# Moving the column transform and the tile sum to later places in TensorE's order

## The chip, the cores and the metric

The kernel runs on one core of a Trainium2 chip. Its time is the device time of one execution in microseconds (us). The kernel before takes 4047.03 us (median of three runs, 4043.34 to 4052.0).

## The reference

Eight images of 8 channels and 256 x 256 pixels go through a Fourier layer network and then through a dilation. Cut to what matters here:

```python
h = _gconv1x1(h, fc0_w, fc0_b)
for i in range(4):
    h1 = _spectral_conv(h, sp_w1[i], sp_w2[i])   # rfft2, mix of 2 x 12 x 12 modes, irfft2
    h2 = _gconv1x1(h, w_w[i], w_b[i])            # 4 groups of 10 channels
    h = h1 + h2
    if i < 3:
        h = _gswish(h, betas[i])
h = _gswish(_gconv1x1(h, fc1_w, fc1_b), betas[3])   # 10 -> 128 per group
return _gconv1x1(h, fc2_w, fc2_b)                   # 128 -> 2 per group
...
x = x + _L0_conv_ref(_gn(x), ...)
x = x + _L1_conv_ref(_gn(x))     # maximum over 3 x 3 windows
```

The kernel does the transforms as matrix products with cosine and sine tables. Within the loop over layers each pixel chunk of layer l gets its new values, and at once the row-wise (width) part of the forward transform that layer l + 1 needs: this is what the change moves.

## The kernel before

An image has 11 chunks of pixels (`NCH = 11`). For layers 0 to 2 each chunk goes through these parts:

- `burst(c)`, TensorE: 16 matmuls of the 1x1 convolution (L480, in layer 0 L477) and 8 of the inverse transform (L483) into two PSUM tiles; ScalarE then applies SiLU into `h` (L489).
- `turn(c)`, VectorE: transposes the chunk in 32 x 32 blocks into one of three slots of `turned` (L431).
- `transform(k)`, TensorE: for pair k (chunks 2k and 2k + 1) 32 matmuls of 32 x 32 into two PSUM tiles (L448), copied to `e` in a slot of `turned`, one by VectorE (L201) and one by ScalarE (L199).
- `gather(k)`, TensorE: four matmuls with stacked unit matrices that sum the four row tiles of `e` (L462), copied to `zt` by VectorE (L465 or L468). This is the tile sum.

```python
def ps_z(name):
    return ps.tile([128, 2, 512], F32, tag="z", bufs=4, name=name)
...
def transform(k):
    cs = chunks_of(k)
    ...
    pair = [ps_z(f"p_d_{b}_{l}_{k}_{i}") for i in range(2)]
    for v in range(8):
        for q in range(NQ):
            mm(pair[q // 2][part(v % 4), q % 2, : 240 * n], fw8[part(q), v, :],
               t[part(q), :, :, v, : NBLK * WID], start=v < 4, stop=v >= 4)
    e = turned[:, (2 * k + 1) % 3, : 960 * n].rearrange("p (q x) -> p q x", q=NQ)
    for i in range(2):
        copy_2(i, e[:, 2 * i : 2 * i + 2], pair[i][:, :, : 240 * n])

def gather(k):
    ...
    e = turned[:, (2 * k + 1) % 3, : 960 * n].rearrange("p (q r f i) -> p q r f i", q=NQ, r=2 * n, f=NQ)
    p = ps_a(f"p_u_{b}_{l}_{k}")
    for g in range(NQ):
        m = e[:, :, :, g] if group_in_f else e[:, g].rearrange("p q r i -> p r q i")
        mm(p[part(g), : 240 * n], stack, m, start=True, stop=True)
    ...

def burst(c):
    pair = [ps_z(f"p_z_{b}_{l}_{c}_{i}") for i in range(2)]
    for f in range(NQ):
        for q in range(NQ):
            o = pair[q // 2][part(f), q % 2, :]
            ...
                mm(o, wt[part(q), l, g, :], h[part(q), c, f, :], start=True, stop=False)
    for s in range(2):
        for q in range(NQ):
            mm(pair[q // 2][:, q % 2, HW * s : HW * (s + 1)],
               zt[part(q), 2 * c + s].rearrange("p f o -> p (f o)"), binv[part(q), :],
               start=False, stop=s == 1)
    for i in range(2):
        ...
            nc.scalar.activation(dst, pair[i], AF.Silu)
```

`ps_a` is the first bank of a `ps_z` tile. [...] While image b + 1 goes through the layers, the head of image b (fc1 and fc2) and its dilation run in between: each `yield` of a layer hands over to the main loop, which puts in steps of the head.

```python
for n in layers(b, stored, d, start(b + 1, ahead)):
    if isinstance(n, str):                 # "even"/"odd": bring the count of steps to that parity
        if count[0] % 2 != (n == "odd") and step():
            share -= 1.0
    elif isinstance(n, tuple):             # (1,): one step exactly, and a bit of the dilation
        exact += sum(n)
        for _ in range(sum(n)):
            if scale and step():
                tail()
    else:                                  # a number: a share of a step
        loose += n
        share += n * scale if scale else 0
        while share >= 1.0:
            share -= 1.0
            step()
scale = scale or (STEPS - exact) / loose   # STEPS = 128 steps per image
```

In image 0 there is no head yet, and no step is put in. An odd step is `first(n)`: 4 matmuls of fc1 (L628) into two PSUM tiles, with SiLU by ScalarE (L630). An even step is `second(n - 4)`, 8 matmuls of fc2 (L650) whose result VectorE adds to `y` (L655), and then a `first(n)`. In the trace an fp32 matmul has two rows, so fc1 is x8, fc2 x16, the transform x64, the tile sum x8.

Of the kernel before, what the change touches and what calls it, by code (L numbers as in the profile page):

```python
# [33 lines left out]
NCH = 11  # L34
# [10 lines left out]
def fno_dilate_kernel(ctx: ExitStack, tc: tile.TileContext, a: dict, out: bass.AP):  # L45
# [10 lines left out]
    def ps_z(name):  # L56
        return ps.tile([128, 2, 512], F32, tag="z", bufs=4, name=name)

    def ps_a(name):
        return ps_z(name)[:, 0, :]  # L60

    def part(i):
        return slice(32 * i, 32 * i + 32)
# [133 lines left out]
    def copy_2(i, dst, src):  # L197
        if i % 2:
            nc.scalar.activation(dst, src, AF.Identity)  # L199
        else:  # L200
            nc.vector.tensor_copy(dst, src)  # L201
# [146 lines left out]
    def load_sw(l, k):  # L348
        t = sb.tile([128, G, 2 * WID, WID], F32, tag="sw")
        nc.sync.dma_start(t.rearrange("p g m i -> p (g m i)"), a["spw"][l, k])  # L350
        return t
# [72 lines left out]
    def layer(b, l, out_, stored, side):  # L424
        group_in_f = l % 2 == 1

        def turn(c):

            dst = turned[:, c % 3].rearrange("p (s f x) -> p f s x", s=2, f=NQ)
            for i in range(2):  # L430
                nc.vector.transpose(  # L431
                    dst[:, 2 * i : 2 * i + 2], h[:, c, 2 * i : 2 * i + 2].rearrange("p f (s x) -> p f s x", s=2))

        def chunks_of(k):

            return sorted(range(2 * k, min(2 * k + 2, NCH)), key=lambda c: c % 3)

        def transform(k):


            cs = chunks_of(k)
            n, lo = len(cs), cs[0] % 3
            step = cs[-1] % 3 - lo if n == 2 else 1
            t = turned[:, lo : lo + step * (n - 1) + 1 : step].rearrange("p n (r v i) -> p n r v i", r=2 * NQ, v=8)
# [12 lines that stand above are left out]
            n = len(cs)  # L457
# [5 lines that stand above are left out]
            src = p[:, : 240 * n].rearrange("p (r g i) -> p r g i", r=2 * n, g=G)  # L463
            if cs == sorted(cs):
                nc.vector.tensor_copy(zt[:, 4 * k : 4 * k + 2 * n, :, : NBLK * WID], src)  # L465
            else:
                for i, c in enumerate(cs):
                    nc.vector.tensor_copy(zt[:, 2 * c : 2 * c + 2, :, : NBLK * WID], src[:, 2 * i : 2 * i + 2])  # L468
# [6 lines that stand above are left out]
                    if l == 0:  # L475
                        k = slice(32 * q, 32 * q + 6)
                        mm(o, wcn[k, :], h[k, c, f, :], start=True, stop=False)  # L477
                    else:
                        g = f if group_in_f else q
# [7 lines that stand above are left out]
                dst = h[:, c, 2 * i : 2 * i + 2, :]  # L487
                if l < 3:
                    nc.scalar.activation(dst, pair[i], AF.Silu)  # L489
                else:  # L490
                    nc.scalar.activation(dst, pair[i], AF.Identity, bias=bias3)  # L491
            if l == 3:
                nc.sync.dma_start(stored[c], h[:, c].rearrange("p f w -> p (f w)"))
# [19 lines left out]
                yield (LAST,)  # L513
            return
        yield "even"
        for c in range(NCH):
            k = c // 2
            if c % 2 == 0:
                burst(c)
                yield (1,)  # L520
                turn(c)
                if k > 0:
                    transform(k - 1)
            else:
                burst(c)
                if k > 0:
                    gather(k - 1)
                yield (1,)
                turn(c)
        out_["sw"] = [load_sw(l + 1, 0), load_sw(l + 1, 1)]  # L530
        yield 1
        gather(k - 1)
        transform(k)
        yield 2
# [10 lines left out]
    def layers(b, stored, d, then):  # L545

        for l in range(4):  # L550
            if l > 0:
                yield from spectrum_h(b, l, d)
                yield from mix(b, l, d)
            yield from rows_of(b, l)
            yield from layer(b, l, d, stored, then if l == 3 else iter(()))
        yield from then
# [367 lines left out]
```

## Time and profile before

| engine | busy us | share of the span |
|---|---|---|
| TensorE, matmul (PE) | 3734.7 | 92% |
| TensorE, weight load (PEld) | 1463.3 | 36% |
| ScalarE (ACT) | 2853.1 | 71% |
| VectorE (DVE) | 2538.8 | 63% |
| GpSimd (POOL) | 117.0 | 3% |

The profiled execution spans 4041.6 us at a mean TensorE clock of 0.977 of full speed. The costliest groups of instructions:

| line | engine | what | count | busy us | mean ns |
|---|---|---|---|---|---|
| L630 | ScalarE | SiLU behind fc1 | 2048 | 1960.1 | 1026 |
| L628 | TensorE | fc1 | 8192 | 1204.4 | 631 |
| L650 | TensorE | fc2 | 8192 | 997.5 | 601 |
| L431 | VectorE | turn | 528 | 623.2 | 1219 |
| L483 | TensorE | burst, inverse transform | 5632 | 411.7 | 405 |
| L480 | TensorE | burst, 1x1 convolution | 8448 | 371.1 | 601 |
| L448 | TensorE | column transform | 9216 | 309.9 | 540 |
| L462 | TensorE | tile sum | 1152 | 137.3 | 546 |
| L201 | VectorE | copy of the transform | 144 | 152.1 | 1057 |
| L199 | ScalarE | copy of the transform | 144 | 130.1 | 903 |

Busy time of overlapping matmuls is the time in which at least one of a group runs, so the busy times of lines are not additive. A mean of a line mixes its shapes: the last transform of a layer has one chunk only, and half the columns. How long TensorE is kept by a group of matmuls is read from the start of the group to the start of the next.

### The profile page before, as it was taken

How to read it: one execution, taken by the hardware profiler on the slowest of the kernel's cores; microseconds unless marked ns; L12 is line 12 of the kernel's file. 1: busy time of each engine (PE TensorE's matmuls, PEld its weight loads, DVE VectorE, ACT ScalarE, POOL GpSimd, SP SyncE). 2: the span in 40 equal slices, each digit the busy share in tenths (PEclk: the TensorE clock that was granted, in tenths of full speed). 3: DMA queues.
4: the chain of work that ended last, by engine and by line, in shares of the span. 5: the costliest groups of instructions: out<-in, count | busy, mean ns of one | idle time of the engine just before them, and what ended most of it. 6: DMA issues, size and time to landing. Idle time of an engine off the chain costs nothing.

```text
span 4041.6 us, 118640 instructions
## 1 busy us (share of the span) xinstructions
PE 3734.7 (92%) x53530; PEld 1463.3 (36%) x53530; DVE 2538.8 (63%) x3535; ACT 2853.1 (71%) x2991; POOL 117.0 (3%) x202
## 2 busy tenths in 40 slices
PE   5666999999999999999999999999999999999997
PEld 2333333433333333333433333333333333333221
DVE  6765656556766666766666666666676666673533
ACT  3334777777777777777777777777777777778886
POOL 1000000000000000000000000000000000000000
PEclk8888999999999999999999999999999999999998
DMA  3005111432125321252122611144121532215311
GB/s 85 14 14 188 53 33 41 139 123 58 58 67 166 93 59 58 82 189 56 55 64 89 197 44 53 53 134 151 55 59 51 164 109 63 61 48 194 96 53 46
DMA packets 113985, 345.05 MB, mean 85 GB/s; under 512 B 15768, under 2 KB 18392, under 8 KB 98056
## 3 DMA queue, kind: packets, MB, share of 16 engines
q1 hardware_dynamic: 95288, 276.33, 22.0%
q0 software_dynamic: 18192, 61.13, 4.7%
q8 instruction: 422, 6.91, 0.7%
q14 instruction: 83, 0.68, 0.1%
HBM read 213.40 MB, written 123.74 MB: 83 GB/s over the span
## 4 chain that ended last, share of the span: by engine, by line
PE 78%; DVE 11%; ACT 7%; issue 3%; DMA 1%; POOL 0%; DVEq 0%; POOLq 0%; SPq 0%; ACTq 0%
PE p_fc L650 22%; PE p_fc L628 20%; PE p_z L483 8%; PE p_z L480 7%; PE p_d L448 6%; ACT act L630 4%; PE p_u L462 3%; PE p_z L477 3%; DVE turned L431 2%; PE p_b L333 2%; PE p_g L405 2%; PE p_g L410 2%; ACT h L491 2%; DVE turned L324 2%; DVE turned L201 1%
## 5 line engine op out<-in xcount | busy, mean ns | idle before, releaser
L630 ACT ACTIVATE act<-p_fc 128x1024 f32<-128x1024 f32 x2048 | 1960.1, 1026 | 669.6 <-PE p_fc L628 665.3
L628 PE MATMUL p_fc<-hs,c_w 32*128 32x512 f32 x8192 | 1204.4, 631 | 14.8 <-DVE turned L195 8.5
L650 PE MATMUL p_fc<-act,c_w 128*32 128x512 f32 x8192 | 997.5, 601 | 47.1 <-ACT act L630 35.5
L628 PEld LDWEIGHTS p_fc<-hs,c_w 32*128 32x128 f32 x8192 | 402.3, 183 | 697.3 <-ACT act L630 278.5
L489 ACT ACTIVATE h<-p_z 128x1024 f32<-128x1024 f32 x528 | 511.7, 1021 | 190.5 <-PE p_z L483 189.8
L431 DVE STREAM_TRANSPOSE turned<-h 128x1024 f32<-128x1024 f32 x528 | 623.2, 1219 | 23.4 <-ACT h L489 23.1
L655 DVE TENSOR_TENSOR y<-p_fc,y 128x512 f32<-128x512 f32 x392 | 270.6, 690 | 497.1 <-PE p_fc L650 496.1
L650 PEld LDWEIGHTS p_fc<-act,c_w 128*32 128x32 f32 x8192 | 227.5, 109 | 645.6 <-issue 345.5
L483 PE MATMUL p_z<-c_binv,zt 32*128 32x256 f32 x5632 | 411.7, 405 | 0.6 <-ACT zt L193 0.6
L480 PE MATMUL p_z<-h,c_wt 32*32 32x512 f32 x8448 | 371.1, 601 | 6.7 <-DVE y L655 3.4
L483 PEld LDWEIGHTS p_z<-c_binv,zt 32*128 32x128 f32 x5632 | 261.6, 186 | 305.4 <-issue 295.8
L448 PE MATMUL p_d<-turned,c_fw 32*32 32x480 f32 (+1 forms) x9216 | 309.9, 540 | 11.1 <-DVE turned L431 11.1
L195 DVE COPY zt<-p_g 128x264 f32<-128x264 f32 x300 | 162.6, 629 | 167.1 <-PE p_g L410 91.6
L491 ACT ACTIVATE h<-p_z,c_bias 128x1024 f32<-128x1024 f32 x176 | 186.5, 1111 | 38.8 <-PE p_z L483 38.4
L199 ACT ACTIVATE turned<-p_d 128x960 f32<-128x960 f32 x144 | 130.1, 903 | 94.5 <-PE p_d L448 94.5
L363 DVE TENSOR_REDUCE S<-turned 128x80 f32<-128x800 f32 x192 | 188.8, 983 | 4.7
L448 PEld LDWEIGHTS p_d<-turned,c_fw 32*32 32x32 f32 x9216 | 121.5, 103 | 187.1 <-issue 150.6
L360 DVE TENSOR_TENSOR turned<-t,B 128x800 f32<-128x800 f32 x192 | 188.6, 982 | 0.9 <-DMA t<-in_spw 0.8
L462 PE MATMUL p_u<-turned,c_stack 128*32 128x480 f32 (+1 forms) x1152 | 137.3, 546 | 42.9 <-DVE turned L201 42.9
L324 DVE STREAM_TRANSPOSE turned<-zt 128x960 f32<-128x960 f32 x96 | 175.6, 1857 | 0.6
L201 DVE COPY turned<-p_d 128x960 f32<-128x960 f32 x144 | 152.1, 1057 | 28.9 <-PE p_d L448 28.7
L480 PEld LDWEIGHTS p_z<-h,c_wt 32*32 32x32 f32 x8448 | 93.7, 103 | 211.2 <-ACT act L630 69.1
(169 smaller groups left out, 1964.8 us busy)
## 6 DMA issues: line engine op xcount, KB each, us to landing
stored<-h SPq DMA_DIRECT2D x88, 1024.0 KB
hs<-stored SPq DMA_DIRECT2D x352, 256.0 KB
t<-in_spw SPq DMA_DIRECT2D x96, 400.0 KB
yin<-y_rows POOLq DMA_DIRECT2D x56, 512.0 KB, 5.0
h<-in_xp SPq DMA_DIRECT2D x352, 48.0 KB
turned<-in_x SPq DMA_DIRECT2D x16, 1024.0 KB
y<-in_x SPq DMA_DIRECT2D x56, 256.0 KB
y_rows<-y POOLq DMA_DIRECT2D x56, 256.0 KB, 2.3
```

The source lines that it names most:

```text
L324: nc.vector.transpose(rows[:, 960 * g : 960 * (g + 1)].rearrange("p (i r) -> p i r", r=32), windows(g))
L431: nc.vector.transpose(dst[:, 2 * i : 2 * i + 2], h[:, c, 2 * i : 2 * i + 2].rearrange("p f (s x) -> p f s x", s=2))
L448: mm(pair[q // 2][part(v % 4), q % 2, : 240 * n], fw8[part(q), v, :], t[part(q), :, :, v, : NBLK * WID], start=v < 4, stop=v >= 4)
L462: mm(p[part(g), : 240 * n], stack, m, start=True, stop=True)
L480: mm(o, wt[part(q), l, g, :], h[part(q), c, f, :], start=True, stop=False)
L483: mm(pair[q // 2][:, q % 2, HW * s : HW * (s + 1)], zt[part(q), 2 * c + s].rearrange("p f o -> p (f o)"), binv[part(q), :], start=False, s ...
L489: nc.scalar.activation(dst, pair[i], AF.Silu)
L491: nc.scalar.activation(dst, pair[i], AF.Identity, bias=bias3)
L628: mm(pair[g // 2][:, g % 2, :], w1[part(g), blk, :], hs[k][part(g), :], start=True, stop=True)
L630: nc.scalar.activation(act[:, 2 * i : 2 * i + 2, :], pair[i], AF.Silu)
L650: mm(acc[part(g), :], w2[:, g, 15 - rb - i : 47 - rb - i], act[:, g, :], start=i == 0, stop=i == 1)
L655: nc.vector.tensor_tensor(y, sums, y, ALU.add)
```

## The change

Before, the transform of a pair stood behind the first burst of the next pair, and its tile sum behind the second burst. Now the transform stands behind the second burst of the next pair, and the tile sum behind the first burst of the pair after that, just ahead of the even step and so of fc2. The transform then has one burst more in which the turn of its chunks can end, and the tile sum has a step and a burst between the copies of `e` and itself. The slots of `turned` allow it: the slot that `turn(2k)` fills is the one that `gather(k - 2)` has just read.

Two things follow from the loop over pairs: the last pair (one chunk) now also has two exact steps, so that a layer has 12 where it had 11, and the share of a step (`yield 1`) ahead of the last two tile sums falls away.

```diff
         yield "even"
-        for c in range(NCH):
-            k = c // 2
-            if c % 2 == 0:
-                burst(c)
-                yield (1,)
-                turn(c)
-                if k > 0:
-                    transform(k - 1)
-            else:
-                burst(c)
-                if k > 0:
-                    gather(k - 1)
-                yield (1,)
-                turn(c)
+        for k in range((NCH + 1) // 2):
+            c = 2 * k
+            burst(c)
+            if k > 1:
+                gather(k - 2)
+            yield (1,)
+            turn(c)
+            if c + 1 < NCH:
+                burst(c + 1)
+            if k > 0:
+                transform(k - 1)
+            yield (1,)
+            if c + 1 < NCH:
+                turn(c + 1)
         out_["sw"] = [load_sw(l + 1, 0), load_sw(l + 1, 1)]
-        yield 1
         gather(k - 1)
         transform(k)
         yield 2
         gather(k)
         yield 1
```

Line numbers from L530 on are smaller by one in the changed kernel: fc1 is L627 there, fc2 L649.

## The prediction

> **What bounds the kernel now.** I began with the page: busy time of each engine and the slices.
>
> ```profile
> PE 3734.7 (92%) x53530; PEld 1463.3 (36%) x53530; DVE 2538.8 (63%) x3535; ACT 2853.1 (71%) x2991; POOL 117.0 (3%) x202
> ...
> PE   5666999999999999999999999999999999999997
> ...
> PE 78%; DVE 11%; ACT 7%; issue 3%; DMA 1%; POOL 0%; DVEq 0%; POOLq 0%; SPq 0%; ACTq 0%
> ```
>
> TensorE is busy for 90% or more in every slice but the first four and the last; the third line, from the chain of work that ended last, puts 78% of the span on it. So only TensorE's own sequence counts, except in the first 400 us, where image 0 runs without a head to interleave. A busy row does not tell whether TensorE streams or waits inside a group, so I went on to the timeline of TensorE in layer 0 of image 2. Columns: start, duration, engine, line, operation. Read the differences of starts, because the durations overlap.
>
> ```profile
> 1380.63 2.19 PE L448 MATMUL p_d<-turned,c_fw 32*32 32x480 f32 x61
> 1382.27 0.59 PE L477 MATMUL p_z<-h,wcn 6*32 6x512 f32 x1
> 1382.28 0.59 PE L448 MATMUL p_d<-turned,c_fw 32*32 32x480 f32 x3
> 1382.48 1.45 PE L477 MATMUL p_z<-h,wcn 6*32 6x512 f32 x31
> 1383.86 1.15 PE L483 MATMUL p_z<-c_binv,zt 32*128 32x256 f32 x16
> 1384.94 1.02 PE L462 MATMUL p_u<-turned,c_stack 128*32 128x480 f32 x8
> 1385.89 1.36 PE L628 MATMUL p_fc<-hs,c_w 32*128 32x512 f32 x8
> 1387.18 1.14 PE L477 MATMUL p_z<-h,wcn 6*32 6x512 f32 x32
> 1388.25 1.16 PE L483 MATMUL p_z<-c_binv,zt 32*128 32x256 f32 x16
> 1389.34 1.92 PE L650 MATMUL p_fc<-act,c_w 128*32 128x512 f32 x16
> 1391.19 1.14 PE L628 MATMUL p_fc<-hs,c_w 32*128 32x512 f32 x8
> 1392.27 2.19 PE L448 MATMUL p_d<-turned,c_fw 32*32 32x480 f32 x61
> ```
>
> This is one pair of chunks: transform (L448), second burst (L477, L483), tile sum (L462), fc1 (L628), first burst of the next pair, fc2 (L650), fc1. From start to start: transform and the burst's first half 3.23 us together, L483 1.08, L462 0.95, fc1 1.29, L477 1.07, L483 1.09, fc2 1.85, fc1 1.08. Sum 11.64, and most pairs of images 1 to 7 repeat 11.63. The only visible wait inside is 0.22: fc1 behind L462 takes 1.29, other fc1 groups 1.07.
>
> Two other places have larger waits. First, the end of a layer, in the timeline of all engines:
>
> ```profile
> 1416.18 2.24 PE L448 MATMUL p_d<-turned,c_fw 32*32 32x480 f32 x64
> ...
> 1418.46 1.16 DVE L201 COPY turned<-p_d 128x960 f32<-128x960 f32 x1 [0.24 <-PE p_d L448]
> ...
> 1419.76 1.01 PE L462 MATMUL p_u<-turned,c_stack 128*32 128x480 f32 x8 [1.34 <-DVE turned L201]
> ...
> 1537.78 2.24 PE L448 MATMUL p_d<-turned,c_fw 32*32 32x480 f32 x64
> ...
> 1539.95 1.14 PE L628 MATMUL p_fc<-hs,c_w 32*128 32x512 f32 x8
> 1541.36 1.01 PE L462 MATMUL p_u<-turned,c_stack 128*32 128x480 f32 x8 [0.27 <-DVE turned L201]
> ```
>
> The fifth tile sum needs the copies of the fifth transform. In the first three lines (layer 0) nothing lies between and it starts 3.58 us after the transform; in the last three (layer 1) an fc1 lies between, and it starts at the same distance, 3.58. So the fc1 there is free. Second, image 0:
>
> ```profile
> 86.58 2.19 PE L448 MATMUL p_d<-turned,c_fw 32*32 32x480 f32 x61 [0.68 <-DVE turned L431]
> ...
> 95.02 2.19 PE L448 MATMUL p_d<-turned,c_fw 32*32 32x480 f32 x61 [0.74 <-DVE turned L431]
> ```
>
> A pair takes 8.4 us; the transform waits for VectorE's turn of the chunk just before.
>
> [...] digit 9 stands over groups that contain the 0.22. [...] L483 (32*128) before fc1 of the same mode takes 0.97, before another mode 1.07 to 1.09, so a switch costs about 0.11. [...] every group waits for the release four allocations earlier. [...]
>
> **The change, part by part.** No instruction is added or removed; the built order of TensorE has as many rows as before. A pair becomes burst, tile sum, fc2, fc1, burst, transform, fc1.
>
> (a) Steady pair, images 1 to 7. Terms: transform up to fc1 2.17 (1537.78 to 1539.95 above); fc1 1.07; L477 1.07; L483 1.08; L462 0.95; fc2 1.85; fc1 1.07; L477 1.07; L483 1.08. Sum 11.41. L462 and fc2 share the mode 128*32, so I take off 0.11 for the saved switch (my estimate from L483's difference): 11.30. The 0.22 behind L462 is gone, as fc2's accumulator has long been free. Against this stands a new wait. The burst after the transform's fc1 now gets the two PSUM tiles that the transform filled; the built program shows its first matmuls waiting for ScalarE and the third for VectorE. The VectorE copy begins 2.28 after the transform's start and takes 1.16, so ends at 3.44; with the passage to TensorE (0.14, from 1419.62 to 1419.76) the third matmul starts at 3.58, where it could have started at 3.24. That is 0.34, the same distance at which L462 follows in layer 1 (1.41 for an fc1 instead of 1.07). 11.30 + 0.34 = 11.64 against 11.63: nothing. Four such pairs in each of 21 layers, about 1 us in all, which I round to +2.
>
> (b) End of a layer. The pair loop now always ends with a step, so an fc1 stands between transform 4 and tile sum 4 in all layers; before, only in layer 1 of each image (read from the order of both programs). The head's steps per stage stay as many, so this fc1 leaves a place where it cost 1.07. Two layers in each of seven images: 14 x 1.07 = 15 us saved.
>
> (c) Late pairs. Where the dilation of the previous image puts more work ahead of the copy on VectorE, a pair took 11.7 to 11.9, and 12.2 at the end of layer 0. The first transform gap of layer 0 in image 2 was 12.70. After the change the tile sum stands a whole burst and two steps behind its copies, and such lateness can hide. I count a modest 5 us saved.
>
> (d) Image 0, no steps. Sum of a pair: L477 1.07 + L483 1.08, twice, + L462 0.95 + transform 2.15 = 7.40. The transform's turn was issued before the previous transform's end, so the 0.7 us wait goes. A PSUM wait of about 0.15 stays, because the second burst's second tile is freed by the first burst's SiLU, 1.17 after that burst, while L462 covers 0.95. So 7.5 against 8.38. Four gaps save 3.5 to 4.4 per layer; the last turn, now later on VectorE, gives back 0.6. About 3.7 in each of three layers: 11 us.
>
> Sum: +2 - 15 - 5 - 11 = -29; 4047 - 29 = 4018.
>
> **Rivals.** Rival 1: the new wait for the transform's copies is larger, because VectorE comes late to them (turn, fc2's sum and dilation work in the same queue). For it: at the end of layer 2 in the later images transform to tile sum took 4.68 instead of 3.58. Against it: in the new order the fc2 sum and the turn of the first chunk have a second burst of 2.15 more before the copy is due. At 0.5 more per pair on 84 pairs: +42, total about 4060. Rival 2: [...] the moved fc1 does not save its 1.07 because the stage that it left was itself waiting, and only image 0 gains: about 4036. Rival 3: the 0.34 is hidden, because the first two matmuls of the burst cover it, and avoided switches save more than 0.11: 84 x 0.4 = 34 more, about 3985. I chose the middle since its terms are read from starts that exist in the trace.
>
> **Range and chances.** Between rival 3 and rival 2 with some slack for the spread of the runs before (4043 to 4052): 3996 to 4042. Two per cent is 81 us, below 3966; that needs twice of rival 3's gain. Faster by over 2%: 0.04; within 2%: 0.95; slower: 0.01, as rival 1 would need 1 us per pair.
>
> **What would show it.** Right: pairs of 11.6 in images 1 to 7 and 7.5 in image 0; fc1's 1.29 behind L462 gone; the burst's first half after the transform's fc1 at about 1.4 instead of 1.07; transform 4 to tile sum 4 at 3.6 with an fc1 between, in all layers. Wrong: steady pairs that differ from 11.63 by more than 0.2, which makes 17 us per 0.2; image 0 still at 8.4; or step-laden stages that grow by what the ends of layers lose.

## The result, and the profile after

The changed kernel takes 4004.52 us (median of four runs, 4002.96 to 4007.91) beside 4045.59 us of the kernel before in the same runs: a ratio of 0.9897, 95% interval 0.9880 to 0.9914, or 42 us (35 to 49) less. Run again on another occasion it gave 0.9889 (0.9874 to 0.9903). The forecast was 4018, 29 us less, in a range from 3996 to 4042.

The page of the changed kernel, in the views shown of before (fc1 is L627 here, fc2 L649):

```profile
PE 3727.3 (93%) x53530; PEld 1447.4 (36%) x53530; DVE 2539.7 (63%) x3535; ACT 2853.2 (71%) x2991; POOL 117.0 (3%) x202
...
PE   5667999999999999999999999999999999999997
...
PE 4%; ACT 1%; DVE 1%; issue 0%; DMA 0%; DVEq 0%; POOLq 0%; POOL 0%
```

TensorE has the same 53530 rows of matmuls and 7 us less of busy time; the span is 40 us shorter, so most of the gain is idle time of TensorE, not work. The mean granted clock is 0.977 in both profiles, so the clock has no part in it. The slices look almost the same, which shows how little they resolve. The shares of the chain add up to some 6% only: here the chain was followed back over the last stretch alone, and it can't be set beside the chain of before.

One pair of chunks in the timeline of TensorE, at the place that the prediction shows of before (start, duration, operation; read the differences of starts). Counted from image 0, it is layer 0 of image 3; the prediction calls it image 2:

```profile
1366.12 2.24 PE L448 MATMUL p_d<-turned,c_fw 32*32 32x480 f32 x64
1368.29 1.14 PE L627 MATMUL p_fc<-hs,c_w 32*128 32x512 f32 x8
1369.42 1.33 PE L477 MATMUL p_z<-h,wcn 6*32 6x512 f32 x32
1370.68 1.15 PE L483 MATMUL p_z<-c_binv,zt 32*128 32x256 f32 x16
1371.76 1.01 PE L462 MATMUL p_u<-turned,c_stack 128*32 128x480 f32 x8
1372.59 1.90 PE L649 MATMUL p_fc<-act,c_w 128*32 128x512 f32 x16
1374.42 1.14 PE L627 MATMUL p_fc<-hs,c_w 32*128 32x512 f32 x8
1375.49 1.18 PE L477 MATMUL p_z<-h,wcn 6*32 6x512 f32 x32
1376.60 1.15 PE L483 MATMUL p_z<-c_binv,zt 32*128 32x256 f32 x16
1377.68 2.24 PE L448 MATMUL p_d<-turned,c_fw 32*32 32x480 f32 x64
```

From start to start: 2.17, 1.13, 1.26, 1.08, 0.83, 1.83, 1.07, 1.11, 1.08, in all 11.56 against 11.63 before. The tile sum beside fc2 takes 0.83 where it took 0.95. But fc1 and L477 behind the transform take 1.13 and 1.26, where each took 1.07 before: 0.25 of new wait, and the other L477 takes 1.11, 0.04 more. The named change is almost a draw in a steady pair.

The end of a layer (first three lines) and image 0 (last two), in the same view:

```profile
1398.61 2.24 PE L448 MATMUL p_d<-turned,c_fw 32*32 32x480 f32 x64
...
1400.78 1.14 PE L627 MATMUL p_fc<-hs,c_w 32*128 32x512 f32 x8
...
1402.19 1.02 PE L462 MATMUL p_u<-turned,c_stack 128*32 128x480 f32 x8 [0.27 <-DVE turned L201]
...
86.56 2.19 PE L448 MATMUL p_d<-turned,c_fw 32*32 32x480 f32 x61
...
94.19 2.19 PE L448 MATMUL p_d<-turned,c_fw 32*32 32x480 f32 x61
```

From the fifth transform to the fifth tile sum it is 3.58, with an fc1 between, and 3.58 or 3.59 in all 21 layers of images 1 to 7. In image 0 a pair takes 7.63 instead of 8.4, and the wait for VectorE's turn in the brackets is gone.

Laid side by side, the two traces differ by 40 us: about 12 of it in image 0, about 24 from the last burst of a layer to the next layer's first in images 1 to 7 (the tile sum that has moved past the last burst taken out, at 0.95 each), about 5 from the first burst of a layer to its last.

### The profile page after: what moved, and what is told of

It is laid out like the page before. It is cut to its first block, busy times and chain, and to the rows that moved or that the text cites. A ratio compares the mean times of both kernels' runs of the same rounds, so it can differ in the third digit from the quotient of the medians.

```text
span 4001.2 us, 118518 instructions
## 1 busy us (share of the span) xinstructions
PE 3727.3 (93%) x53530; PEld 1447.4 (36%) x53530; DVE 2539.7 (63%) x3535; ACT 2853.2 (71%) x2991; POOL 117.0 (3%) x202
## 5 line engine op out<-in xcount | busy, mean ns | idle before, releaser
L627 PE MATMUL p_fc<-hs,c_w 32*128 32x512 f32 x8192 | 1187.5, 631 | 16.2 <-DVE turned L195 8.4
L649 PE MATMUL p_fc<-act,c_w 128*32 128x512 f32 x8192 | 997.4, 601 | 47.7 <-ACT act L629 37.2
L627 PEld LDWEIGHTS p_fc<-hs,c_w 32*128 32x128 f32 x8192 | 389.1, 183 | 700.5 <-ACT act L629 292.9
L649 PEld LDWEIGHTS p_fc<-act,c_w 128*32 128x32 f32 x8192 | 235.5, 110 | 664.1 <-issue 397.7
L483 PE MATMUL p_z<-c_binv,zt 32*128 32x256 f32 x5632 | 410.3, 404 | 0.7 <-ACT zt L193 0.6
L483 PEld LDWEIGHTS p_z<-c_binv,zt 32*128 32x128 f32 x5632 | 259.1, 186 | 304.8 <-issue 294.4
L480 PE MATMUL p_z<-h,c_wt 32*32 32x512 f32 x8448 | 353.1, 602 | 8.8 <-DVE y L654 5.1
L480 PEld LDWEIGHTS p_z<-h,c_wt 32*32 32x32 f32 x8448 | 83.2, 103 | 231.2 <-issue 62.1
```

What stands on the lines that cost most here:

```text
L483: mm(pair[q // 2][:, q % 2, HW * s : HW * (s + 1)], zt[part(q), 2 * c + s].rearrange("p f o -> p (f o)"), binv[part(q), :], start=False, s ...
L627: mm(pair[g // 2][:, g % 2, :], w1[part(g), blk, :], hs[k][part(g), :], start=True, stop=True)
L649: mm(acc[part(g), :], w2[:, g, 15 - rb - i : 47 - rb - i], act[:, g, :], start=i == 0, stop=i == 1)
```

## The experiments

Each ratio is to the kernel before, run beside it on the same chip; 0.001 is 4 us. All kernels compute the whole reference.

**Image 0 alone.** The new loop only where `b == 0`, the old loop elsewhere:

```diff
+        if b == 0:
+            for k in range((NCH + 1) // 2):   # the new loop
+                ...
+        else:
             for c in range(NCH):              # the old loop
                 ...
-        yield 1
+        if b > 0:
+            yield 1
```

> The new order in image 0 alone, the old order in images 1 to 7. Theory (image 0 has nothing between its bursts, so its gain is TensorE's wait for the turn and stays to the end): pairs of 7.6 us instead of 8.4 in image 0, about 12 us less than before, near 4033; images 1 to 7 keep pairs of 11.63. Rival (what image 0 gains is lost again later, as the rest of the program is bound otherwise): the time of before, 4045.

Measured: 4032.72, ratio 0.9954 (0.9942 to 0.9967), 19 us less (13 to 24). But the share of a step is worked out in image 0, which here counted 12 exact steps a layer, and in the trace steps of images 1 to 7 stood elsewhere. So a second form has 11 exact steps and the `yield 1` in image 0 too, and there TensorE's order in images 1 to 7 is that of before:

> The new order in image 0 alone, this time with the 11 exact steps and the share of a step of the old order there, so that the share of a step, which is worked out in image 0, stays as it was and TensorE's order in images 1 to 7 is the old one to the letter. Theory: 12 to 14 us less than before, near 4033, and nothing else changed. Rival (part of the first run's gain came from steps placed otherwise in images 1 to 7): image 0 gives under 8 us.

Measured: 4036.72, ratio 0.9958 (0.9943 to 0.9973), 17 us less (11 to 23). The rival's under 8 is excluded. Image 0 gives its part by itself.

**The end of the layer alone.** The old order, with one exact step where a share of a step stood:

```diff
                 if k > 0:
                     transform(k - 1)
+                if c == NCH - 1:
+                    yield (1,)
...
-        yield 1
         gather(k - 1)
```

> The old order, with one exact step between the fifth transform and the fifth tile sum in every layer, in place of the share of a step that stood there. Theory (the fc1 there is free, and also hides the late copies of layer 2): 1.1 us less in layer 0 and 2.4 us less in layer 2 of each of 7 images, about 24 us less than before, near 4021. First form of the theory, as predicted: 15 us less, near 4030. Rival (a step costs the same wherever it stands): 4045.

Measured: 4023.03, ratio 0.9933 (0.9920 to 0.9945), 27 us less (22 to 32). This is two thirds of the whole gain, without moving transform or tile sum at all. It is also more than the 15 us of the forecast. The difference is in layer 2. First the kernel before, layer 2 of image 2, then the changed kernel at the same place:

```profile
1179.91 0.69 DVE L655 TENSOR_TENSOR y<-p_fc,y 128x512 f32<-128x512 f32 x1 [1.00 <-PE p_fc L650]
1180.52 0.54 DVE L706 TENSOR_SCALAR o<-o,mr_y 128x512 f32<-128x512 f32 x1
1180.84 2.24 PE L448 MATMUL p_d<-turned,c_fw 32*32 32x480 f32 x64
...
1181.36 0.69 DVE L713 TENSOR_TENSOR o<-o,yin 128x512 f32<-128x512 f32 x1
1181.97 2.36 DVE L431 STREAM_TRANSPOSE turned<-h 128x1024 f32<-128x1024 f32 x2
...
1184.26 1.12 DVE L201 COPY turned<-p_d 128x960 f32<-128x960 f32 x1
1185.52 1.01 PE L462 MATMUL p_u<-turned,c_stack 128*32 128x480 f32 x8 [2.44 <-DVE turned L201]
```

```profile
1162.81 0.69 DVE L654 TENSOR_TENSOR y<-p_fc,y 128x512 f32<-128x512 f32 x1 [1.06 <-PE p_fc L649]
1163.42 2.36 DVE L431 STREAM_TRANSPOSE turned<-h 128x1024 f32<-128x1024 f32 x2
1163.74 2.24 PE L448 MATMUL p_d<-turned,c_fw 32*32 32x480 f32 x64
...
1166.02 1.16 DVE L201 COPY turned<-p_d 128x960 f32<-128x960 f32 x1 [0.24 <-PE p_d L448]
...
1167.33 1.02 PE L462 MATMUL p_u<-turned,c_stack 128*32 128x480 f32 x8 [0.27 <-DVE turned L201]
```

Before, dilation work (L706 to L713) stood between fc2's sum and the turn on VectorE, the copy began 3.42 after the transform's start instead of 2.28, and the tile sum came at 4.68. In the changed kernel no dilation work stands there. A part of the dilation is handed out with each exact step, and a layer has 12 of them instead of 11, so another part of it meets the end of the layer. In the experiment, as in the changed kernel, the distance is 3.58 or 3.59 in every layer.

**The change without its end step.** The counterpart: the new order, with 11 exact steps and the share of a step.

```diff
-            yield (1,)
             if c + 1 < NCH:
+                yield (1,)
                 turn(c + 1)
...
+        yield 1
         gather(k - 1)
```

> The new order with 11 exact steps in a layer and the share of a step ahead of the last two tile sums, as before: fc1 stands between the fifth transform and its tile sum in layer 1 alone. Theory (the end of the layer gives more than half of the gain, the same as in the old order): 22 to 27 us over the new order, near 4028, with the fifth tile sum 3.6 us or later behind its transform without an fc1 between. Rival (in the new order the pairs bring the gain and the end of the layer is hidden): within 8 us of the new order.

Measured: 4034.74, ratio 0.9960 (0.9948 to 0.9973), 26 us over the changed kernel by the two ratios. The trace has 3.58 in layer 0 and again 4.68 in layer 2 of images 2 to 7, with no fc1 between; here in image 5:

```profile
2621.38 2.24 PE L448 MATMUL p_d<-turned,c_fw 32*32 32x480 f32 x64
2626.06 1.82 PE L462 MATMUL p_u<-turned,c_stack 128*32 128x480 f32 x8 [2.44 <-DVE turned L201]
2627.81 2.06 PE L448 MATMUL p_d<-turned,c_fw 32*32 32x240 f32 x64
```

So the lateness of VectorE in layer 2 comes with the count of steps, not with the order of transform and tile sum. The 26 us are not this wait and the fc1 alone: in five of the six images the tile sum behind it took 1.6 to 1.8 to the next start instead of 0.95, and the mean granted clock of the runs was 0.973 to 0.975 beside 0.975 to 0.978 in the changed kernel, some 12 us by an estimate from the two means. That they came out as expected is in part luck. Set beside image 0 alone (0.9958), this kernel differs from it by the new order in images 1 to 7, and gains nothing that these intervals show (each is about 5 us wide to either side, and its lower clock may hide a few us). The two parts multiply: 0.9933 x 0.9958 = 0.9891, against 0.9897 measured for the whole.

**Only the tile sum moved.** The transform goes back ahead of the second burst:

```diff
-            if c + 1 < NCH:
-                burst(c + 1)
             if k > 0:
                 transform(k - 1)
+            if c + 1 < NCH:
+                burst(c + 1)
             yield (1,)
```

> The tile sum at its new place ahead of fc2, two exact steps for the last pair, but the transform at its old place ahead of the second burst. Theory (what counts is which group of matmuls comes two double PSUM tiles later: here only an fc1 of 1.07 lies between the second burst and the next first burst, whose third matmul must wait for the second burst's last SiLU, 2.04 after its end): about 1.0 us of wait in every pair, pairs of 12.3 instead of 11.56, with image 0 near its old 8.4: about 70 us over the new order, near 4075. Rival (the tile sum beside fc2, which saves a mode switch, brings the gain): within 10 us of the new order.

Measured: 4090.12, ratio 1.0098 (1.0085 to 1.0112), 81 us over the changed kernel. Its TensorE timeline, second burst, fc1 and next first burst:

```profile
1414.04 1.15 PE L483 MATMUL p_z<-c_binv,zt 32*128 32x256 f32 x16
1415.00 1.21 PE L627 MATMUL p_fc<-hs,c_w 32*128 32x512 f32 x8
1416.29 2.05 PE L477 MATMUL p_z<-h,wcn 6*32 6x512 f32 x32
1418.28 1.15 PE L483 MATMUL p_z<-c_binv,zt 32*128 32x256 f32 x16
```

L477 takes 1.99 to the next start instead of 1.11, and the pair 12.28 (transform at 1410.81 to transform at 1423.09). L477 is the group that was named to wait, and by about the time named. The tile sum still takes 0.84 beside fc2 (1419.35 to 1420.19), so the saved mode switch is there and is about a seventh of what the wait costs (0.12 of 0.88). On 84 pairs 0.72 is 60 us; in layer 0 some pairs took 13.9 (in the one from 1396.90 to 1410.81, L483 took 1.89 to the next start instead of 1.07 and the tile sum 1.60 instead of 0.84), and the mean granted clock of the runs was 0.970 to 0.973 beside 0.975 to 0.978 in the changed kernel, some 20 us by an estimate from the two means. In image 0, where I had expected some 8.4, a pair took 7.89.

**Only the transform moved.** The tile sum of the same pair directly behind the step:

```diff
             burst(c)
-            if k > 1:
-                gather(k - 2)
             yield (1,)
...
             if c + 1 < NCH:
+                if k > 0:
+                    gather(k - 1)
                 turn(c + 1)
```

> The transform at its new place behind the second burst, two exact steps for the last pair, but the tile sum already behind the fc1 that follows it, ahead of the next first burst and not behind it. Theory (the tile sum then waits 0.35 for the copies, and the burst's third matmul about 0.9 for the fc1's SiLU, since only the tile sum of 0.95 lies between): pairs of 12.6 to 12.7 instead of 11.56, pairs of about 9.0 in image 0: about 105 us over the new order, near 4110. Rival (the transform behind the second burst brings the gain, the tile sum's place matters little): within 10 us of the new order.

Measured: 4048.20, ratio 0.9995 (0.9987 to 1.0004), 40 us over the changed kernel. Neither the expected 105 nor the rival's 10:

```profile
1402.82 2.24 PE L448 MATMUL p_d<-turned,c_fw 32*32 32x480 f32 x64
1404.99 1.14 PE L627 MATMUL p_fc<-hs,c_w 32*128 32x512 f32 x8
1406.40 1.01 PE L462 MATMUL p_u<-turned,c_stack 128*32 128x480 f32 x8 [0.27 <-DVE turned L201]
1407.35 1.15 PE L477 MATMUL p_z<-h,wcn 6*32 6x512 f32 x32
1408.42 1.16 PE L483 MATMUL p_z<-c_binv,zt 32*128 32x256 f32 x16
```

The wait of the tile sum is there (1404.99 to 1406.40 is 1.41), the burst's expected 0.9 is not: L477 takes 1.07. I had given the burst's second PSUM tile the release by fc1's second SiLU. In the trace the SiLUs of this fc1 end at 1407.25 and 1408.17, and the burst's third matmul starts at 1407.36: it did not wait for the second one. The pair takes 11.80, 0.24 over the changed kernel, which is 20 us on 84 pairs; in image 0, where no fc1 covers the copies, layers 1 and 2 took about 6 us more each, and layer 0 took 20 more in this profile, at a mean granted clock of 0.71 from its first burst to that of layer 1, instead of 0.83 (70.08 to 152.2 in the changed kernel). The tile sum's place thus matters, though less than the transform's.

**Both copies of the transform on VectorE:**

```diff
             for i in range(2):
-                copy_2(i, e[:, 2 * i : 2 * i + 2], pair[i][:, :, : 240 * n])
+                copy_2(0, e[:, 2 * i : 2 * i + 2], pair[i][:, :, : 240 * n])
```

> The new order with both copies of a transform on VectorE, one behind the other, where ScalarE took one. Theory (the next first burst gets the PSUM tiles of the transform, so it waits for their copies, though the tile sum needs them much later): the second copy ends at about 4.56 instead of 3.44 after the transform's start, 1.1 us more in every pair of images 1 to 7, pairs of 12.6, about 90 us over the new order. Rival (the copies have a burst and two steps of slack ahead of the tile sum): within 10 us of the new order.

Measured: 4157.63, ratio 1.0272 (1.0256 to 1.0288), 152 us over the changed kernel.

```profile
1421.60 2.24 PE L448 MATMUL p_d<-turned,c_fw 32*32 32x480 f32 x64
1423.77 1.14 PE L627 MATMUL p_fc<-hs,c_w 32*128 32x512 f32 x8
1425.10 2.29 PE L477 MATMUL p_z<-h,wcn 6*32 6x512 f32 x32 [0.18 <-DVE turned L201]
1427.32 1.15 PE L483 MATMUL p_z<-c_binv,zt 32*128 32x256 f32 x16
```

L477 takes 2.22 and the pair 12.72, 1.16 more, as the theory has it: 97 us on 84 pairs. The copies are on TensorE's path through the PSUM tiles that they free, although the tile sum that reads their result comes a burst later and takes 0.83 as ever. The remaining 50 or so the expectation had left out. By the trace, the last transform of a layer comes 5.5 to 5.6 behind the fifth instead of 4.53, about 1 us in each of 21 layers; image 0 takes 11 us more; and in layer 0 some pairs took 14.2 or more (in the one from 1407.36 to 1421.60, L483 took 2.01 instead of 1.08), about 20 us in all; the mean granted clock of the runs was 0.965 to 0.971.

**The burst's matmuls by PSUM tile**, so that the tile with the later release is written from the 9th matmul on:

```diff
-            for f in range(NQ):
-                for q in range(NQ):
+            for f, q in [(f, 2 * i + u) for i in range(2) for f in range(NQ) for u in range(2)]:
+                if True:
                     o = pair[q // 2][part(f), q % 2, :]
```

> The new order, with the 16 matmuls of a burst's first half ordered by PSUM tile, so that the tile which waits for VectorE's copy of the transform is first written by the 9th matmul and not by the 3rd. Theory (in the new order the burst behind the transform's fc1 waits some 0.2 us at its third matmul for VectorE's copy): the group takes about 1.07 instead of 1.26, the pair 11.36 to 11.40 instead of 11.56, 84 pairs, 13 to 17 us less than the new order, near 3989. Rival ([...] the copies come so late that 9 matmuls do not cover it): 4004.

> The old order with the same reordering of the burst's matmuls: the control of the run above. Theory (in the old order no burst waits for a transform's copy, its only wait in the pair is fc1's behind the tile sum): no change, 4045 within 4. Rival (the order by tile is better for TensorE by itself): some 15 us less, as in the run above.

Measured: 0.9875 (0.9861 to 0.9888) in the new order, 0.9998 (0.9991 to 1.0004) in the old one. In the trace of the first, L477 behind the transform's fc1 and then an undisturbed one:

```profile
1376.97 1.28 PE L477 MATMUL p_z<-h,wcn 6*32 6x512 f32 x32
1378.18 1.15 PE L483 MATMUL p_z<-c_binv,zt 32*128 32x256 f32 x16
...
1382.99 1.22 PE L477 MATMUL p_z<-h,wcn 6*32 6x512 f32 x32
1384.14 1.15 PE L483 MATMUL p_z<-c_binv,zt 32*128 32x256 f32 x16
```

1.21 instead of 1.26 and 1.15 instead of 1.11: what is gained in one burst is mostly lost in the other. A pair takes 11.55 in layer 0 and 11.51 in layers 1 and 2 instead of 11.56, about 3 us on 84 pairs, and the expected 13 to 17 us are missed. The ratio hinted at 9 us all the same. Three more runs side by side decide it: the changed kernel, the form with only the waiting bursts by tile, and the first form again.

> The changed kernel itself once more, on the same chip as the runs beside it, as their base. Expected: ratio 0.9897 as measured, 4004 to 4009.

> The new order, with the matmuls by PSUM tile only in the bursts of chunks 4, 6, 8 and 10, which wait for the transform's copies, and the old order of matmuls in all others (where the order by tile was seen to cost 0.04 us in each burst). Theory: 1.21 instead of 1.26 in those bursts and 1.11 in the others, 0.05 us in 84 pairs, 4 us less than the changed kernel. Rival (the order by tile brings 9 us, as the run with all bursts suggested): as that run, about 4000.

> The new order with all bursts by PSUM tile, as in the third run, once more beside the changed kernel on one chip. Theory (by the trace 0.05 us gained and 0.04 lost in each pair): within 3 us of the changed kernel. Rival (the 9 us of difference between the two ratios are real): 6 to 12 us less than the changed kernel.

Measured: 0.9889 (0.9874 to 0.9903), 0.9890 (0.9875 to 0.9905) and 0.9894 (0.9878 to 0.9910). All three are the same within their intervals, and the 9 us were not repeated. No version here beats the changed kernel.

## Why the prediction was right, step by step

- **(a) Steady pair.** Put at 11.64, measured 11.56; by the trace 84 x 0.07 = 6 us saved where +2 was put, and nothing that the runs resolve. The mechanism held: the 0.22 behind the tile sum goes, a wait for the transform's copies comes. The mis-sized term is that wait, 0.34 in the sum and 0.25 in the trace. VectorE's copy ends at 3.44 behind the transform's start, as put, but the burst's third matmul starts at 3.49 and not at 3.58: the passage takes 0.05 there, where 0.14 was taken over from the tile sum. The saved mode switch was put at 0.11 and is 0.12: the tile sum, 128*32 in the rows, took 0.95 ahead of fc1 (32*128) and takes 0.83 ahead of fc2 (128*32).
- **(b) End of a layer.** Put at 15, measured 27 (22 to 32). The step held in its kind, but it counted only the fc1 that becomes free. In layer 2 of images 2 to 7 the tile sum also comes 1.1 earlier (4.68 to 3.58), 6 x 1.1 = 7 us. From the fifth transform to the next layer's first burst the trace of the run with the end step alone is 24 us shorter than that of before, as is that of the changed kernel. What makes up the last few us of the 27 I have not isolated; the interval reaches down to 22.
- **(c) Late pairs.** Put at 5 us in the pairs. Half of it held. In images 1 to 7 of the trace before, the gaps between transforms other than the first of layer 0 had 5.9 us above 11.63 in all (12.2 at the end of layer 0, 11.7 to 11.9 elsewhere). In the changed kernel 0.5 is left of this, and in the run without the end step 0.3, so the new order does hide such lateness. But the first gap of layer 0, which the prediction named with its 12.70, stays: 12.68 in four images, 12.25 in one and 14.24 in image 3 (see the last section), 1.4 us more in all, and the way from the first burst of layer 0 to its first transform took 4.8 us more than the burst that moved into it. So (c) came to nothing. The lateness of VectorE that cost most was at the end of layer 2, and it went with the count of steps.
- **(d) Image 0.** Put at 11, measured 17 (11 to 23); about 10 to 14 by the traces. Pairs of 7.5 were put and 7.63 found.
- **The rivals.** Rival 1, VectorE late to the copies in every pair, did not come. Rival 2 fell with the end-step run: a step moved to the waiting place does save its time. Rival 3, the wait hidden by the burst's first matmuls, did not come either: the wait was 0.09 shorter than put because the passage was, and an order of matmuls that would hide more of it gained nothing.

Sum by the traces: 6 in the steady pairs, 24 at the ends of the layers, 12 in image 0 and about -1 for (c), 41 us, against 42 measured. The forecast of 29 was low through steps (b) and (a), and (c), put 5 too high, hid a part of that: that it came as near as it did is in part luck.

## What to carry to other kernels

When groups of matmuls share a ring of PSUM tiles, ask of each new order which group comes into a tile next and how long the copy or activation that frees it takes; with only one of the two groups moved, the kernel took 81 and 40 us more than with both. Test a change's small print apart from its headline: here one more step at the end of a layer, which came along with the new loop, made two thirds of the gain. And an op that is free where it stands (an fc1 inside a wait) is worth more than a saved wait that another one replaces: here 27 us at the ends of the layers, and by the trace 6 in the steady pairs.

## What the runs showed of the hardware

In one place what followed a short wait cost more than the wait: by the starts 1.40 us behind a wait of 1.29. In layer 0 of image 3 of the changed kernel, fc1 waited 0.38 us, and some 0.9 more inside the group (1.97 to the next start instead of 1.07), for SiLUs that stood behind two activation-table loads of ScalarE, 1.28 us each (from 1350.61 and 1352.13). The busy times of TensorE, its weight loads, VectorE, ScalarE and GpSimd in stretches around it, then the granted clock, DMA share and GB/s:

```profile
1354.40:1357.00 2.60, 2.50 (x36) 0.83 (x40) 2.60 (x4) 2.60 (x5) 0.00 (x0) 1.00 0.00 0
1357.00:1361.00 4.00, 4.00 (x56) 1.62 (x28) 0.65 (x1) 2.20 (x4) 0.00 (x0) 0.57 0.02 4
1361.00:1365.00 4.00, 4.00 (x60) 0.94 (x52) 2.65 (x4) 1.70 (x2) 0.00 (x0) 1.00 0.00 0
```

Some 3 us after the wait the granted clock fell, to 0.50 from 1357.3 to 1360.7 and so to a mean of 0.57 over the 4 us of the second line, and the groups in that stretch took longer (L483 2.02 to the next start instead of 1.08, the tile sum 1.29 instead of 0.83): the pair came to 14.24 instead of 11.56. The stretch of the same 3.4 us before, 1353.9 to 1357.3, was not idle: TensorE shows 3.02 of 3.40 us busy in it at a granted clock of 1.00, with the waits inside the groups counted as busy. Whether the waits set it off was not tried, and the length of a wait does not decide it alone: within 3 us of the start of the 2.44 us wait at the end of layer 2 the granted clock fell to 0.50 in one of six images of the kernel before (image 4, from 2150.7 to 2154.1, where the tile sum took 1.76 to the next start instead of 0.95). In the run without the end step the tile sum behind that wait took 1.6 to 1.8 in five of six images; that its clock fell there too is an estimate from these lengths beside the 1.76.
